# One 192-column PSUM bank for half B's three gate sums in a gated recurrent layer

## The chip, the cores and the metric

The kernel runs on one core of one Trainium2 chip. The metric is the device time of one execution in microseconds (us), and lower is better. Before the change it is 1670.06 us, the median of 3 runs.

## The reference

A gated recurrent layer walks 512 steps over 8 sequences of width 512, and its states are added to its input:

```python
def step(h, x_t):
    fused = sigmoid(concatenate([x_t, h], -1) @ w_W + w_b)
    hidden_state, output_state = split(fused, 2, axis=-1)          # r, z
    memory_state = x_t @ wx_W + wx_b + hidden_state * (h @ wh_W + wh_b)
    h_new = output_state * h + (1.0 - output_state) * tanh(memory_state)
    return (h_new, h_new)
return x + swapaxes(scan(step, h0, swapaxes(x, 0, 1))[1], 0, 1)
```

All arrays are float32: x is (8, 512, 512), w_W is (1024, 1024), wx_W and wh_W are (512, 512). The state of one step is needed by every product of the next one, so the steps form a chain.

## The kernel before

**Halves.** The 512 units lie as four chunks of 128. Chunks 0 and 1 are half A, chunks 2 and 3 half B. Each half has its own state tile (`hTA`, `hTB`), its own gates and its own place in the order of work. Three sums are wanted per step and half: hh (the product with wh_W), z and r, each 64 columns wide.

**TensorE.** For every step i the product of the state with the weights is issued as groups named by a bank and a chunk k of the state: A0 multiplies chunk 0 into bank A. A group is four matmuls, one for each j, and each writes 32 of the 128 output partitions, so four run beside each other. Each matmul of the program stands in the trace as two records (8176 records of `A<-wa,hTA` are 511 steps times 16, for the 8 matmuls of A0 and A1). Chunks 0 and 1 come from `hTA`, chunks 2 and 3 from `hTB`. The order is written out by hand:

```python
ORDER = "A0 B0 A1 A2 A3 B1 B2 B3 C0 C1 C2 C3"
BANKS = {"A": 192, "B": 128, "C": 64}
```

Bank A holds hh, z, r of half A (192 columns). For half B, bank B holds r and hh (128 columns) and bank C holds z (64 columns). After C3, `take(later, 7)` issues seven matmuls of 192 columns of the x side (tile `xp`), which belong to later steps and wait for no state. They are used up in steps 5 to 500; the last 11 steps have none, and steps 0 to 4 have wider ones of another kind (384 columns). `turn` rotates the order of j, so that the four strips share the x side evenly over the steps.

**VectorE and ScalarE.** Both work through a fixed order, the order of the source. In each step VectorE does, with the names of the trace:

1. half A: `tr<-A` (transpose of r), `md1A<-A` (of hh), `tz<-A` (of z), then two scans `m<-md0A,md1A` that make the memory state of chunks 0 and 1;
2. half B: `tr<-B`, `md1B<-B`;
3. the scan `hTA<-hd0A,hTA` of chunk 0, the new state that A0 and B0 of the next step wait for;
4. half B: `tz<-C`;
5. the scan `hTA` of chunk 1, then two scans `m` of half B and two scans `hTB`, for which A2 and A3 of the next step wait;
6. a few steps of upkeep (a transpose of the x side, memsets).

ScalarE takes the sigmoids (`md0A<-tr`, `hd0A<-tz` and the same for B) and the tanh (`hTA<-m`, `hTB<-m`) between them, and at the end of a step copies. A wait in this order holds up all that stands behind it on the engine. In the code the steps are `turn_r`, `turn_h`, `turn_z`, `memory` and `update`, each called for half 0 (A) and 1 (B); their transposes are recorded at L374 and L390, the scans at L358, the activations at L216, and every matmul at L188.

**Banks and spreads.** Each of the banks exists twice, and four steps (a group g) accumulate in one set. Before a group begins, `spread` copies the x part of its sums from `xp` (or from a copy in SBUF) into its banks on ScalarE (L251). There is one such copy for each bank and group. GpSimd adds x to the new state and SyncE stores the rows.

Of the kernel before, what the change touches and what calls it, by code (L numbers as in the profile page):

```python
# [16 lines left out]
B = 8  # L17
HU = 64
# [5 lines left out]
LAST = 4  # L24
SYNC = mybir.DependencyInfo(mybir.DependencyClass.Sync, mybir.DependencyReason.DATA)

ORDER = "A0 B0 A1 A2 A3 B1 B2 B3 C0 C1 C2 C3"

FIRST = "A0 x A1 x A2 x A3 B0 B1 B2 B3 C0 C1 C2 C3"

BANKS = {"A": 192, "B": 128, "C": 64}

HALF = 192

AL, BE = (0, slice(64, 256)), (0, slice(256, 448))
GA, DE = (1, slice(64, 256)), (1, slice(256, 448))

XP = {"A": slice(0, 192), "X": slice(192, 320), "C": slice(320, 384), "B": slice(384, 512)}


@with_exitstack
def tile_cond_rnn_residual(
# [84 lines left out]
    wa = const.tile([P, NQ, NQ, 192], F32, name="wa")  # L127
    for k in range(NQ):
        nc.sync.dma_start(out=wa[:, k], in_=wa_d[k])
    wb = const.tile([P, NQ, NQ, 192], F32, name="wb")  # L130
# [1 line left out]
    nc.sync.dma_start(out=wb[:, 3], in_=wb3_d)  # L132

    def wh(bank, k, j):
        return wa[:, k, j] if bank == "A" else wb[:, k, j, {"C": slice(0, 64), "B": slice(64, 192)}[bank]]

    load_x(0, 1)

# [36 lines left out]
    def state(hf, i, slot=2):  # L175
# [5 lines left out]
    banks = [  # L181
        {n: psum.tile([P, w], F32, name=f"{n}{q}") for n, w in BANKS.items()}
        for q in range(2)
# [3 lines left out]
    def mm(out_, lhsT, rhs, start=False):  # L187
        nc.tensor.matmul(  # L188
            out_, lhsT, rhs, start=start, stop=False, skip_group_check=True
        )  # L190
# [31 lines left out]
    def seed(g):  # L222

        nc.scalar.copy(xps[g % 2], bias)  # L224
# [19 lines left out]
    def part(g, c0, c1):  # L244

        return late(g)[:, c0 - 256 : c1 - 256] if c0 >= 256 else xps[g % 2][:, c0:c1]

    def spread(g, names):

        for n in names:  # L250
            nc.scalar.copy(banks[g % 2][n], part(g, XP[n].start, XP[n].stop))  # L251

    def turn_x(g, e):

        c0 = XP["X"].start + 32 * e
        nc.vector.transpose(md1[e // 2][g % 2][:, :, e % 2, 1], part(g, c0, c0 + 32))

    def reg(r):
        return xps[r[0]][:, r[1]]
# [8 lines left out]
    def weight_sum(n, k=slice(0, 2), j=None):  # L268

        a, b = [  # L270
            (wx_of(0, 1), wx_of(0, 0)),
            (wx_of(1, 1), tw[0]),
            (wx_of(1, 1), wx_of(0, 1)),
            (wx_of(1, 0), tw[1]),
        ][n]
        at = (slice(0, P), k, slice(0, NQ) if j is None else slice(2 * j, 2 * j + 2))
        nc.vector.tensor_tensor(tw[n][at], a[at], b[at], ALU.subtract)

    def x_sum(o, n):

        t_ = [q[o % 2] for q in sx]
        a, b, op = [
            (x_half(o, 1, 0), x_half(o, 1, 1), ALU.add),
            (t_[0], x_half(o, 0, 0), ALU.subtract),
            (x_half(o, 0, 0), x_half(o, 1, 0), ALU.subtract),
            (x_half(o, 0, 1), t_[1], ALU.subtract),
        ][n]
        nc.gpsimd.tensor_tensor(t_[n], a, b, op)
# [32 lines left out]
    first = {g: prefill(g) for g in (1, 2, 3)}  # L321
    weight_sum(0)
    weight_sum(2)
    spread(0, "BCA")
    for e in range(NQ):
        turn_x(0, e)

# [1 line left out]
    for i in range(T):  # L329
        g, s = divmod(i, GS)  # L330
        c, t = divmod(i, TC)
        ps = banks[g % 2]
# [4 lines left out]

        for n in (ORDER if i else FIRST).split():
            if n == "x":
                take(first[1], 1)  # L340
                continue
            bank, k = n[0], int(n[1])
            hs = hT[k // 2][i % NH][:, :, k % 2, 2]
            for j in range(NQ):
                j = (j + turn[0]) % NQ
                to = ps[bank] if i or bank != "A" else xps[0][:, XP["A"]]
                mm(to[32 * j : 32 * j + 32, :], hs, wh(bank, k, j))
# [8 lines left out]
        def scan(c_, out_, d0, d1):  # L356
# [7 lines left out]

        pa = ps["A"] if i else xps[0][:, XP["A"]]
        raw = {
            "h": (pa[:, :HU], ps["B"][:, HU:]),
            "z": (pa[:, HU : 2 * HU], ps["C"]),
            "r": (pa[:, 2 * HU :], ps["B"][:, :HU]),
        }  # L370

        def turned(n, hf):
# [82 lines left out]
        o, u = divmod(i, 2 * GS)  # L455
# [8 lines left out]
        if u == 0:  # L464
            spread(2 * o + 1, "B")
            if o and nxt:
                nc.scalar.copy(reg(GA), reg(BE))
        elif u == 1:
            spread(2 * o + 1, "C")
        elif u == 2 and o == 0:  # L470
            seed(3)
            nc.scalar.copy(even, xps[0][:, 256:512])
        elif u == 2 and nxt:
            last = odd[(o + 1) % 2][:, :HALF]
            nc.vector.tensor_tensor(last, reg(GA), both, ALU.add)
        elif u == 3 and nxt:
            if o:
                nc.vector.tensor_tensor(even[:, :HALF], reg(BE), both, ALU.add)
            spread(2 * o + 2, "A")
        elif u == 4 and nxt:  # L480
            if o == 0:
                nc.scalar.copy(odd[1], xps[1][:, 256:512])
            spread(2 * o + 2, "B")
            if two:
                nc.scalar.copy(reg(AL), bias[:, AL[1]])
                x_sum(o + 2, 0)
        elif u == 5 and nxt:
            spread(2 * o + 2, "C")
            if two:
                nc.scalar.copy(reg(DE), step_bias)  # L490
                x_sum(o + 2, 1)
        elif u == 6 and two:
            nc.scalar.copy(reg(BE), reg(AL))
            x_sum(o + 2, 2)
        elif u == 7 and nxt:
            spread(2 * o + 3, "A")
            if two:
                nc.scalar.copy(both, reg(DE))
                x_sum(o + 2, 3)
# [106 lines left out]
```

## Time and profile before

| what | value |
|---|---|
| median of 3 runs | 1670.06 us (1669.73 to 1671.35) |
| span of the profiled execution | 1670.8 us |
| granted TensorE clock, mean | 0.999 |
| PE busy / PEld busy | 1659.0 us (99%) / 1637.5 us (98%) |
| DVE busy / ACT busy | 1090.5 us (65%) / 1029.9 us (62%) |
| records of matmuls | 56238 |
| idle of DVE ahead of `tr<-A` | 463.5 us in 510 waits |

PE is the matmul side of TensorE and PEld its weight loads; DVE is VectorE, ACT ScalarE. The profiled execution has the span for its time; it is 0.8 us over the median of the runs. A busy PE is not a PE at its peak: the ends of matmuls are modelled and four of them overlap, so a wait of less than a matmul's length does not show as idle time. The starts in the timeline show it.

### The profile page before, as it was taken

What the parts mean: (1) busy time and instruction counts of PE and PEld (TensorE: products, weight loads), DVE (VectorE), ACT (ScalarE), POOL (GpSimd) and SP (SyncE); (2) the same over time, 40 slices, a digit from 0 to 9 for tenths busy, and PEclk for the clock granted to TensorE, in tenths of its full rate; (3) what the DMA queues carried; (4) which work ended last, traced back from release to release, by engine and by line L of the source; (5) the groups of instructions that cost most, each with busy time, mean ns of one, the idle gap of its engine ahead of it and who ended that gap; (6) DMA issues with size and microseconds to landing.
All of it is one profiled execution on the core that took longest, in us unless ns stands there. A gap on an engine that the chain in (4) does not pass through costs nothing.

```text
span 1670.8 us, 129875 instructions
## 1 busy us (share of the span) xinstructions
PE 1659.0 (99%) x56238; PEld 1637.5 (98%) x56238; DVE 1090.5 (65%) x9387; ACT 1029.9 (62%) x5822; POOL 301.9 (18%) x1281
## 2 busy tenths in 40 slices
PE   8999999999999999999999999999999999999998
PEld 5999999999999999999999999999999999999997
DVE  6666666666666666666666666666666666666666
ACT  3666666666666666666666666666666666666665
POOL 1111111111111111111111111111111111111111
PEclk9999999999999999999999999999999999999999
DMA  4000000000000000000000000000000000000000
GB/s 179 17 5 17 18 18 17 17 6 17 17 18 18 5 17 18 17 17 5 18 17 17 18 11 12 18 17 17 18 5 17 17 18 17 5 17 12 11 12 10
DMA packets 11525, 31.40 MB, mean 19 GB/s; under 512 B 1220, under 2 KB 1732, under 8 KB 10824
## 3 DMA queue, kind: packets, MB, share of 16 engines
q1 hardware_dynamic: 10800, 22.94, 4.0%
q8 instruction: 440, 7.21, 1.8%
q14 instruction: 133, 1.09, 0.2%
q10 hardware_dynamic: 152, 0.16, 0.0%
HBM read 14.70 MB, written 8.39 MB: 14 GB/s over the span
## 4 chain that ended last, share of the span: by engine, by line
PE 98%; DVE 1%; DMA 0%; issue 0%; ACT 0%
PE A L188 44%; PE B L188 23%; PE xp L188 20%; PE C L188 12%; DMA rows<-in_bias_dram 0%; DVE tr L374 0%; DVE m L358 0%; DVE tz L374 0%; DVE md1B L390 0%; DVE md1A L390 0%; DVE hTA L358 0%; DVE bias L203 0%; ACT hTB L216 0%; ACT xp L224 0%; DVE rows L120 0%
## 5 line engine op out<-in xcount | busy, mean ns | idle before, releaser
L188 PE MATMUL A<-wa,hTA 128*32 128x192 f32 x8176 | 638.2, 329 | 2.3 <-DVE hTA L358 2.3
L188 PE MATMUL B<-wb,hTA 128*32 128x128 f32 x8192 | 573.8, 273 | 0.0
L188 PE MATMUL A<-wa,hTB 128*32 128x192 f32 x8176 | 507.4, 326 | 0.5 <-DVE hTB L358 0.5
L188 PEld LDWEIGHTS B<-wb,hTA 128*32 128x32 f32 x8192 | 471.2, 122 | 1.4 <-issue 0.2
L374 DVE STREAM_TRANSPOSE tr<-A 128x64 f32<-128x64 f32 x511 | 127.7, 250 | 463.5 <-PE A L188 463.5
L188 PE MATMUL B<-wb,hTB 128*32 128x128 f32 x8192 | 398.9, 273 | 0.0
L188 PEld LDWEIGHTS A<-wa,hTA 128*32 128x32 f32 x8176 | 385.4, 123 | 7.6 <-DVE hTA L358 4.0
L188 PEld LDWEIGHTS A<-wa,hTB 128*32 128x32 f32 x8176 | 372.9, 122 | 2.7 <-DVE hTB L358 0.8
L216 ACT ACTIVATE md0A<-tr 128x16 f32<-128x16 f32 x512 | 112.3, 219 | 421.0 <-DVE tr L374 421.0
L507 POOL TENSOR_TENSOR ot<-xin,hTB 128x16 f32<-128x16 f32 x503 | 125.9, 250 | 1324.5 <-DVE hTB L358 1314.0
L188 PEld LDWEIGHTS B<-wb,hTB 128*32 128x32 f32 x8192 | 321.5, 122 | 0.1
L188 PE MATMUL C<-wb,hTA 128*32 128x64 f32 x8192 | 289.4, 219 | 0.0
L188 PE MATMUL C<-wb,hTB 128*32 128x64 f32 x8192 | 288.9, 220 | 0.2 <-issue 0.2
L188 PEld LDWEIGHTS C<-wb,hTA 128*32 128x32 f32 x8192 | 266.7, 122 | 0.0
L188 PE MATMUL xp<-tw,sx 128*32 128x192 f32 x2976 | 237.2, 326 | 0.1
L188 PEld LDWEIGHTS C<-wb,hTB 128*32 128x32 f32 x8192 | 229.2, 123 | 0.4 <-issue 0.4
L358 DVE TENSOR_TENSOR_SCAN hTB<-hd0B,hTB 128x24 f32<-128x24 f32 x1024 | 157.8, 195 | 101.0 <-ACT hTB L216 99.8
L358 DVE TENSOR_TENSOR_SCAN hTA<-hd0A,hTA 128x24 f32<-128x24 f32 x1024 | 191.0, 187 | 0.0
L188 PE MATMUL xp<-wx,xin 128*32 128x192 f32 (+1 forms) x2048 | 182.4, 331 | 0.7 <-issue 0.5
L216 ACT ACTIVATE hd0B<-tz 128x16 f32<-128x16 f32 x512 | 115.2, 225 | 93.7 <-DVE tz L374 93.7
L216 ACT ACTIVATE hTB<-hTB 128x16 f32<-128x16 f32 x512 | 120.5, 235 | 79.8 <-DVE hTB L358 72.3
L216 ACT ACTIVATE hTB<-m 128x8 f32<-128x8 f32 x1024 | 160.6, 206 | 0.0
(92 smaller groups left out, 2489.6 us busy)
## 6 DMA issues: line engine op xcount, KB each, us to landing
xin<-in_x_dram SPq DMA_DIRECT2D x31, 256.0 KB, 3.5
out_dram<-ot SPq DMA_DIRECT2D x31, 256.0 KB, 2.2
wx<-in_wx_dram SPq DMA_DIRECT2D x4, 768.0 KB, 7.1
wa<-in_wa_dram SPq DMA_DIRECT2D x4, 384.0 KB, 8.9
wb<-in_wb_dram SPq DMA_DIRECT2D x1, 1152.0 KB
wb<-in_wb_dram SPq DMA_DIRECT2D x1, 384.0 KB, 11.1
out_dram<-ot SPq DMA_DIRECT2D x1, 192.0 KB, 3.9
head<-in_xh_dram ACTq DMA_DIRECT2D x1, 144.0 KB, 5.0
```

Source lines behind the costliest of these rows:

```text
L188: nc.tensor.matmul(out_, lhsT, rhs, start=start, stop=False, skip_group_check=True)
L216: inst = nc.scalar.activation(out_, in_, func, **kw).ins
L358: return nc.vector.tensor_tensor_scan(*[t_[:, :, c_].rearrange("p n c s -> p (n c s)") for t_ in (out_, d0, d1)], 0.0, ALU.mult, ALU.add,).ins
L374: inst = nc.vector.transpose(t_.rearrange("p c n -> p (c n)"), raw[n][hf]).ins
L507: return engine.tensor_tensor(ot[:, t, 2 * hf : 2 * hf + 2, :].rearrange("p c n -> p n c"), x_of(c, slice(2 * hf, 2 * hf + 2), t, 1).rearr ...
```

## The change

Half B gets one bank of 192 columns, laid out z, r, hh, as wide as half A's. Bank C goes, and with it the groups C0 to C3 in both orders, the copies into C (128 in all, at steps 1 and 5 of every eight) and the entry for C in the map of `xp`. The matmuls of B are 192 columns wide instead of 128. `tz` of half B reads bank B. The order of all other work stays as it is written.

```diff
-ORDER = "A0 B0 A1 A2 A3 B1 B2 B3 C0 C1 C2 C3"
+ORDER = "A0 B0 A1 A2 A3 B1 B2 B3"
-FIRST = "A0 x A1 x A2 x A3 B0 B1 B2 B3 C0 C1 C2 C3"
+FIRST = "A0 x A1 x A2 x A3 B0 B1 B2 B3"
-BANKS = {"A": 192, "B": 128, "C": 64}
+BANKS = {"A": 192, "B": 192}
-XP = {"A": slice(0, 192), "X": slice(192, 320), "C": slice(320, 384), "B": slice(384, 512)}
+XP = {"A": slice(0, 192), "X": slice(192, 320), "B": slice(320, 512)}
...
-        return wa[:, k, j] if bank == "A" else wb[:, k, j, {"C": slice(0, 64), "B": slice(64, 192)}[bank]]
+        return (wa if bank == "A" else wb)[:, k, j]
...
-    spread(0, "BCA")
+    spread(0, "BA")
...
-            "h": (pa[:, :HU], ps["B"][:, HU:]),
-            "z": (pa[:, HU : 2 * HU], ps["C"]),
-            "r": (pa[:, 2 * HU :], ps["B"][:, :HU]),
+            "h": (pa[:, :HU], ps["B"][:, 2 * HU :]),
+            "z": (pa[:, HU : 2 * HU], ps["B"][:, :HU]),
+            "r": (pa[:, 2 * HU :], ps["B"][:, HU : 2 * HU]),
...
-        elif u == 1:
-            spread(2 * o + 1, "C")
...
-            spread(2 * o + 2, "C")
```

## The prediction

> **What bounds the kernel now.** I read the page's engine shares first, then the waits, then the timeline of single steps, because the first two cannot tell a full TensorE from one that waits in small pieces.
>
> ```profile
> span 1670.8 us, 129875 instructions
> PE 1659.0 (99%) x56238; PEld 1637.5 (98%) x56238; DVE 1090.5 (65%) x9387; ACT 1029.9 (62%) x5822; POOL 301.9 (18%) x1281
> ...
> DVE tr L374 <- PE A L188: 463.5, 510, 1.8
> PEld A L188 <- DVE hTA L358: 4.0, 11, 0.4
> ```
>
> PE is busy throughout, VectorE idles 463.5 / 510 = 0.91 us in each step before `tr<-A`, and TensorE is seen waiting for the state only 11 times. So TensorE's stream sets the time. The period of a step comes from two rows of the timeline, `tr<-A` of steps 5 and 501, with 496 periods between them.
>
> ```profile
> 38.15 0.25 DVE L374 STREAM_TRANSPOSE tr<-A 128x64 f32<-128x64 f32 x1 [1.22 <-PE A L188]
> ...
> 1635.05 0.25 DVE L374 STREAM_TRANSPOSE tr<-A 128x64 f32<-128x64 f32 x1 [0.97 <-PE A L188]
> ```
>
> (1635.05 - 38.15) / 496 = 3.220 us per step. From 1635.05 on there is no x side, and the ten periods up to the last `tr<-A` at 1665.83 (below) take 30.78 / 10 = 3.08 us. These last steps are the key to the case. TensorE has 7 matmuls (14 records) less in them, yet a step is only 0.14 us shorter: there the chain through VectorE and ScalarE sets the time. Here is one of them, from `tr<-A` to the next `tr<-A`.
>
> ```profile
> 1662.73 0.61 PE L188 MATMUL B<-wb,hTB 128*32 128x128 f32 x14
> 1662.75 0.25 DVE L374 STREAM_TRANSPOSE tr<-A 128x64 f32<-128x64 f32 x1 [0.94 <-PE A L188]
> 1663.16 0.41 PE L188 MATMUL C<-wb,hTA 128*32 128x64 f32 x16
> 1663.29 0.28 DVE L358 TENSOR_TENSOR_SCAN m<-md0A,md1A 128x16 f32<-128x16 f32 x2
> 1663.38 0.41 PE L188 MATMUL C<-wb,hTB 128*32 128x64 f32 x16
> 1663.48 0.23 DVE L374 STREAM_TRANSPOSE tr<-B 128x64 f32<-128x64 f32 x1
> 1663.63 0.21 DVE L390 STREAM_TRANSPOSE md1B<-B 128x64 f32<-128x64 f32 x1
> 1663.77 0.20 DVE L358 TENSOR_TENSOR_SCAN hTA<-hd0A,hTA 128x24 f32<-128x24 f32 x1
> 1663.88 0.23 DVE L374 STREAM_TRANSPOSE tz<-C 128x64 f32<-128x64 f32 x1
> 1664.02 0.19 PEld L188 LDWEIGHTS A<-wa,hTA 128*32 128x32 f32 x8 [0.39 <-DVE hTA L358]
> 1664.02 0.55 PE L188 MATMUL A<-wa,hTA 128*32 128x192 f32 x8 [0.24 <-DVE hTA L358]
> 1664.03 0.17 DVE L358 TENSOR_TENSOR_SCAN hTA<-hd0A,hTA 128x24 f32<-128x24 f32 x1
> 1664.23 0.30 PEld L188 LDWEIGHTS B<-wb,hTA 128*32 128x32 f32 x8
> 1664.50 0.25 PEld L188 LDWEIGHTS A<-wa,hTA 128*32 128x32 f32 x8
> 1664.56 0.31 DVE L358 TENSOR_TENSOR_SCAN hTB<-hd0B,hTB 128x24 f32<-128x24 f32 x2 [0.20 <-ACT hTB L216]
> 1664.82 0.58 PEld L188 LDWEIGHTS A<-wa,hTB 128*32 128x32 f32 x16
> 1664.93 0.83 PE L188 MATMUL A<-wa,hTB 128*32 128x192 f32 x16
> 1665.58 0.40 PE L188 MATMUL B<-wb,hTA 128*32 128x128 f32 x8
> 1665.83 0.25 DVE L374 STREAM_TRANSPOSE tr<-A 128x64 f32<-128x64 f32 x1 [0.95 <-PE A L188]
> 1666.24 0.41 PE L188 MATMUL C<-wb,hTA 128*32 128x64 f32 x16
> ```
>
> The chain is `tr<-A` at 1662.75, the scan of `hTA` at 1663.77, the weights of A0 at 1664.02 (1.27 after `tr<-A`), the last matmul of A3 ending at 1664.93 + 0.83 = 1665.76, and `tr<-A` 0.07 later: 1.27 + 1.74 + 0.07 = 3.08. The reader should note that the scan ends at 1663.97 and the weight load follows 0.05 later. A step in the middle of the run has the same front part:
>
> ```profile
> 802.27 0.25 DVE L374 STREAM_TRANSPOSE tr<-A 128x64 f32<-128x64 f32 x1 [1.02 <-PE A L188]
> 803.28 0.20 DVE L358 TENSOR_TENSOR_SCAN hTA<-hd0A,hTA 128x24 f32<-128x24 f32 x1
> 803.54 0.31 PEld L188 LDWEIGHTS A<-wa,hTA 128*32 128x32 f32 x8
> 803.56 0.33 PE L188 MATMUL xp<-wx,sx 128*32 128x192 f32 x2
> ```
>
> Again 803.54 - 802.27 = 1.27 us, 0.06 behind the end of the scan, with x-side matmuls still starting at 803.56. So in the steady state the first weights of A0 are loaded as soon as the state permits, while the x side still fills the other strips. The two limits, stream and chain, lie close together; the chain has about 0.1 us to spare.
>
> **The stream, part by part.** I call four records, one on each strip of 32 partitions, a round. The 16 records of A on `hTB` are four rounds from 1664.93 to 1665.58: 0.163 us a round of 192 columns. The 24 records of B1 to B3 are six rounds from 1665.58 to 1666.24: 0.110 us at 128 columns. The 16 of C on `hTA` are four rounds from 1663.16 to 1663.38: 0.055 us at 64. A B round of 192 columns and the B and C rounds it replaces therefore cost 0.163 against 0.165. Per step 8 rounds of C go (0.44), and 8 rounds of B grow by 0.053 (0.42). TensorE's work shrinks by 0.01 to 0.02 us a step, 32 records and 32 weight loads though it is. Rounding leaves a fixed cost per record between 0 and some 5 ns.
>
> The Trainium skill ("TensorE: Matmul & The Clock Gate", section "Wait — 56ns, not 53.3ns?") names about 2.5 ns fixed per warm matmul. By that rule the eight rounds would give 0.020 us a step, 10 us in all, if TensorE stayed the bound. The rows above cannot tell 1 ns from 2.5, and agree with it in size.
>
> The same skill's "TensorEngine Tiling (Array Packing)", section "Instruction Overhead", says that a matmul costs some 60 cycles however few its columns, which would make 64-column matmuls nearly pure overhead and the merge a large gain. The trace disagrees: 64 columns take 0.055 and 128 take 0.110, in proportion.
>
> **What moves.** The important part is when bank B is complete. Now B1 to B3 end at 1662.73 + 0.61 = 1663.34, well before `tr<-B` at 1663.48, which waits only for VectorE's scans `m`. After the change the z columns are streamed inside B1 to B3 instead of behind them. The last of six rounds starts five times 0.053 later and lasts 0.05 longer, so B ends 0.32 later, at 1663.66. `tr<-B` needs all of bank B. How long it takes from the end of the matmuls to the transpose is shown twice: 0.07 for `tr<-A` above, and in step 0, the only step in which `tr<-B` waited for its matmuls:
>
> ```profile
> 18.46 0.69 PE L188 MATMUL B<-wb,hTB 128*32 128x128 f32 x16
> 19.21 0.25 DVE L374 STREAM_TRANSPOSE tr<-B 128x64 f32<-128x64 f32 x1
> 19.52 0.17 DVE L358 TENSOR_TENSOR_SCAN hTA<-hd0A,hTA 128x24 f32<-128x24 f32 x1
> ```
>
> There it is 19.21 - 19.15 = 0.06, and the scan of `hTA` comes 0.31 behind `tr<-B`, against 1663.77 - 1663.48 = 0.29 where VectorE didn't wait; I take 0.07 and 0.31. `tr<-B` then starts at 1663.73, 0.25 late, and the scan at 0.25 + 0.02 = 0.27 late. Queued behind the waiting `tr<-B` on VectorE are `md1B`, that scan, `tz` of B, the second scan of `hTA`, and all of half B. The order puts the new state of half A behind half B's transposes, so half A, whose inputs are ready, pays for half B's bank.
>
> Next, the release of A0: 1.27 + 0.27 = 1.54 us after `tr<-A`. Would TensorE still have work then? Counted from `tr<-A`: B1 starts 0.25 before it (1665.58 against 1665.83), six rounds of 0.163 take it to 0.73, and four rounds of x side (14 records, so two or four for each strip) to 1.38. Even the strips with most work stand idle for 0.16 us, all four begin A0 together, and the weights aren't loaded ahead: the pattern of the last ten steps. So I take those steps as the template for every step, with A0 0.27 later and B0 of the next step, in front of A1, wider by two rounds of 0.053:
>
> - period: 3.08 + 0.27 + 0.105 = 3.455 us;
> - 496 steps with x side: 496 x (3.455 - 3.220) = 116.6 us;
> - the last ten periods: 10 x (3.455 - 3.08) = 3.8 us; the tail behind the last `tr<-A` 0.3 us;
> - steps 0 to 4 with their wider x side take over 3.9 us now, more than 3.455, so TensorE covers the delay there, at 0.
>
> Sum 120.7 us: 1670.8 + 120.7 = 1791.5 us, and against the median, 0.8 us lower, 1790.7. I forecast 1790.
>
> **What I cost at nothing.** The copies into C go (128 of them, ScalarE, behind the last state of the step) and those into B grow; ScalarE has more idle time than now, and if that cover went, some 0.05 us in every fourth step. A1 waits for the second scan of `hTA`, 1664.03 + 0.17 + 0.27 and 0.06 = 1664.53; its load would come at 1664.50 + 0.27, hidden by 0.24. A2 waits for `hTB`: even the later scan ends at 1664.87 + 0.27, so 1665.20 with the 0.06; its load comes at 1664.82 + 0.27 + 0.11 = 1665.20, just hidden, and the first scan, which is what A2 needs, is earlier. A new wait: B0 writes the bank from which `tz` of B still reads. `tz` would start at 1663.88 + 0.27 and end at 1664.38, 1664.44 with the 0.06; B0's load is due at 1664.23 + 0.27 = 1664.50. It is hidden by 0.06 us, the thinnest cover of all.
>
> On that wait the Trainium skill speaks against the change: "PSUM — Partial Sum Buffer", section "PSUM bank collisions raise a hardware error", has software guard a bank as a whole, so z in the same bank holds back all of B0 and not just z's columns. No row of before shows this wait.
>
> **The rivals.**
>
> 1. *TensorE stays the bound, faster.* Place: the x side between B3 and A0. If A0's state came by 1.38 us after `tr<-A`, the strips would not wait, and only the saved 0.01 to 0.02 us a step would be left: 1660 to 1665 us. It decides if the scan is less than 0.11 us late. For it speaks that the waits show no late state now; against it the sum of 0.27, and that TensorE does stop for 0.24 us in the last steps. Chance 0.04, and 0.01 that it ends within 0.2% of before.
> 2. *The chain is the bound but shorter.* If VectorE follows bank B by 0.04 instead of 0.07, and the strips don't fall into step, so that weights are loaded ahead (in the last steps the A0 records of two rounds and their restart take 1664.39 - 1664.02 = 0.37 to the first of B instead of 2 x 0.163, 0.04 more), the period is 0.07 to 0.09 lower: about 1750 us. Chance 0.13.
> 3. *The new wait of B0 shows.* If the guard against `tz` also keeps the loads behind it from being queued, a cover of 0.06 becomes a stall of about that size, 0.06 x 506 = 30 us: 1820 us. Chance 0.07.
>
> **How the numbers follow.** The forecast has 0.75; with 0.03 us either way on the period it spans 1775 to 1805. The range reaches into rival 2 and toward rival 3: 1748 to 1815. What one measurement can tell from no change is 0.2%, 3.3 us; faster 0.04, same 0.01, slower 0.95.
>
> **What would show it.** In the new profile `tr<-B` should have a wait for PE B in nearly every step and start 0.97 to 1.0 us after `tr<-A` (now 0.73), A0's weights should come at 1.54 (now 1.27) with an idle put down to `hTA`, `tr<-A` should follow itself at 3.45 with and without x side, and the rounds of B should be 0.163. If `tr<-B` waits but the period stays below 3.25, the spare time of the stream was larger than I read; if `tr<-B` doesn't wait, my end of bank B is wrong; if `B` waits for `tz`, rival 3 is at work.

## The result and the profile after

The changed kernel takes 1774.51 us (median of 4 runs, 1773.87 to 1775.2) against 1670.7 us for the kernel before (median of 4 runs, three of which are those behind the 1670.06 us above): a ratio of 1.0617, 95% interval 1.0602 to 1.0632. It is slower, as forecast, by 104 us where the forecast had 120. The two profiled spans differ by 1771.5 - 1670.8 = 100.7 us.

First the page of the changed kernel, then three lines of its waits (us in total, times, longest):

```profile
span 1771.5 us, 96975 instructions
...
PE 1755.4 (99%) x39852; PEld 1370.5 (77%) x39852; DVE 1145.0 (65%) x9387; ACT 1084.1 (61%) x5694; POOL 305.1 (17%) x1281
...
DVE tr L374 <- PE A L188: 427.3, 510, 1.0
PEld A L188 <- DVE hTA L358: 171.1, 507, 1.0
DVE tr L374 <- PE B L188: 83.8, 511, 1.5
```

PE is still 99% busy, with 16386 records of matmuls fewer and 100 us more time: that share cannot tell a stream from a stream with holes, since each matmul's modelled length overlaps its neighbours. The weight loads can. PEld fell from 98% to 77%, and it now waits for the new state of half A in 507 steps instead of 11. `tr<-B` waits for bank B in 511 steps, 0.16 us each; the waits of the kernel before list none for bank B.

One of the last steps in the timeline, which corresponds to the step shown for the kernel before:

```profile
1762.85 0.25 DVE L374 STREAM_TRANSPOSE tr<-A 128x64 f32<-128x64 f32 x1 [1.01 <-PE A L188]
1762.92 0.83 PE L188 MATMUL B<-wb,hTB 128*32 128x192 f32 x16
1763.38 0.28 DVE L358 TENSOR_TENSOR_SCAN m<-md0A,md1A 128x16 f32<-128x16 f32 x2
1763.82 0.25 DVE L374 STREAM_TRANSPOSE tr<-B 128x64 f32<-128x64 f32 x1 [0.16 <-PE B L188]
1763.99 0.21 DVE L390 STREAM_TRANSPOSE md1B<-B 128x64 f32<-128x64 f32 x1
1764.12 0.17 DVE L358 TENSOR_TENSOR_SCAN hTA<-hd0A,hTA 128x24 f32<-128x24 f32 x1
1764.21 0.22 DVE L374 STREAM_TRANSPOSE tz<-B 128x64 f32<-128x64 f32 x1
1764.34 0.19 PEld L188 LDWEIGHTS A<-wa,hTA 128*32 128x32 f32 x8 [0.96 <-DVE hTA L358]
1764.55 0.31 PEld L188 LDWEIGHTS B<-wb,hTA 128*32 128x32 f32 x8
1765.20 0.63 PEld L188 LDWEIGHTS A<-wa,hTB 128*32 128x32 f32 x16
1766.26 0.25 DVE L374 STREAM_TRANSPOSE tr<-A 128x64 f32<-128x64 f32 x1 [1.01 <-PE A L188]
```

Read it from the top. The two scans `m` of half A are over at 1763.66, VectorE stands for 0.16 us until `tr<-B` can start at 1763.82, 0.07 behind the end of the last matmul of bank B (1762.92 + 0.83 = 1763.75), and only then come `md1B` and, third in line, the scan that makes half A's state. A0's weights are loaded at 1764.34, 1.49 us after `tr<-A` (1.27 before). From there to the next `tr<-A` it takes 1.92 us (1.81 before, as B0 now sits there 64 columns wider). 1.49 + 1.92 = 3.41 us is the period, and it is the same with x side: from 38.27 (step 5) to 1732.11 (step 501), 496 periods of 3.415 us.

```profile
38.27 0.25 DVE L374 STREAM_TRANSPOSE tr<-A 128x64 f32<-128x64 f32 x1 [0.94 <-PE A L188]
...
1732.11 0.25 DVE L374 STREAM_TRANSPOSE tr<-A 128x64 f32<-128x64 f32 x1 [0.89 <-PE A L188]
```

### The profile page after: what moved, and what is told of

It reads as the page before. It is cut to its first block, busy times and chain, and to the rows that moved or that the text cites. A ratio compares the mean times of both kernels' runs of the same rounds, so it can differ in the third digit from the quotient of the medians.

```text
span 1771.5 us, 96975 instructions
## 1 busy us (share of the span) xinstructions
PE 1755.4 (99%) x39852; PEld 1370.5 (77%) x39852; DVE 1145.0 (65%) x9387; ACT 1084.1 (61%) x5694; POOL 305.1 (17%) x1281
## 4 chain that ended last, share of the span: by engine, by line
PE 98%; DMA 1%; DVE 0%; ACT 0%; issue 0%
PE A L188 42%; PE B L188 38%; PE xp L188 18%; DMA wb<-in_wb_dram 1%; DMA rows<-in_bias_dram 0%; DVE tr L374 0%; DVE md1B L390 0%; DVE hTA L358 0%; ACT hTB L216 0%; ACT xp L224 0%; DVE rows L120 0%; DVE hTB L358 0%; DVE tz L374 0%; ACT hd0B L216 0%; ACT hTA L216 0%
## 5 line engine op out<-in xcount | busy, mean ns | idle before, releaser
L188 PE MATMUL A<-wa,hTA 128*32 128x192 f32 x8176 | 539.4, 336 | 5.9 <-DVE hTA L358 5.9
L188 PE MATMUL B<-wb,hTA 128*32 128x192 f32 x8192 | 520.5, 326 | 0.8 <-DMA wb<-in_wb_dram 0.8
L188 PE MATMUL B<-wb,hTB 128*32 128x192 f32 x8192 | 426.7, 326 | 0.0
L188 PEld LDWEIGHTS A<-wa,hTA 128*32 128x32 f32 x8176 | 241.6, 124 | 194.3 <-DVE hTA L358 171.1
L188 PEld LDWEIGHTS A<-wa,hTB 128*32 128x32 f32 x8176 | 289.8, 122 | 42.8 <-DVE hTB L358 0.9
L188 PEld LDWEIGHTS B<-wb,hTA 128*32 128x32 f32 x8192 | 289.7, 122 | 42.0 <-DMA wb<-in_wb_dram 1.1
L374 DVE STREAM_TRANSPOSE tr<-B 128x64 f32<-128x64 f32 x512 | 128.0, 250 | 83.8 <-PE B L188 83.8
L216 ACT ACTIVATE md0B<-tr 128x16 f32<-128x16 f32 x512 | 111.2, 217 | 95.0 <-DVE tr L374 94.9
L216 ACT ACTIVATE hTA<-m 128x8 f32<-128x8 f32 x1024 | 160.6, 206 | 0.0
L358 DVE TENSOR_TENSOR_SCAN m<-md0A,md1A 128x16 f32<-128x16 f32 x1024 | 142.0, 181 | 4.4
```

The lines of the kernel that those rows point to most:

```text
L188: nc.tensor.matmul(out_, lhsT, rhs, start=start, stop=False, skip_group_check=True)
L216: inst = nc.scalar.activation(out_, in_, func, **kw).ins
L358: return nc.vector.tensor_tensor_scan(*[t_[:, :, c_].rearrange("p n c s -> p (n c s)") for t_ in (out_, d0, d1)], 0.0, ALU.mult, ALU.add,).ins
L374: inst = nc.vector.transpose(t_.rearrange("p c n -> p (c n)"), raw[n][hf]).ins
```

## The experiments

Below, *release* is the time from `tr<-A` to the first weights of A0 in the next step, and *rest* the time from there to the next `tr<-A`. Theory: the period is the larger of release + rest (the chain) and what TensorE's stream of matmuls needs (the stream), and the change lengthened the release through the late completion of bank B. In the comparisons of this section the kernel before took 1684 to 1688 us and not 1670.7, so each ratio is to the kernel before on the same chip, and absolute times written down beforehand are some 15 us low where the stream decides.

### The same order of columns, with two banks

```diff
-ORDER = "A0 B0 A1 A2 A3 B1 B2 B3 C0 C1 C2 C3"
+ORDER = "A0 B0 C0 A1 A2 A3 C1 C2 C3 B1 B2 B3"
```

> The kernel before with its two banks B (128) and C (64) for half B, but with TensorE's groups in the order A0 B0 C0 A1 A2 A3 C1 C2 C3 B1 B2 B3, which is where the changed kernel has the same columns. Bank B is then complete as late as in the changed kernel, with narrow matmuls and z in a bank of its own. Theory (the loss is the later completion of bank B, which holds up VectorE's transpose of r of half B and, queued behind it, the new state of half A): period about 3.43 us, time about 1784 us (1770 to 1795), tr<-B about 0.99 us after tr<-A. Rival (the shared bank or the 192-column matmuls cost by themselves): near the kernel before, 1670 to 1690 us.

1784.31 us, ratio 1.0593 (1.0576 to 1.0609). Its timeline in the last steps:

```profile
1772.33 0.25 DVE L374 STREAM_TRANSPOSE tr<-A 128x64 f32<-128x64 f32 x1 [1.02 <-PE A L188]
1773.32 0.25 DVE L374 STREAM_TRANSPOSE tr<-B 128x64 f32<-128x64 f32 x1 [0.18 <-PE B L188]
1773.62 0.17 DVE L358 TENSOR_TENSOR_SCAN hTA<-hd0A,hTA 128x24 f32<-128x24 f32 x1
1773.84 0.19 PEld L188 LDWEIGHTS A<-wa,hTA 128*32 128x32 f32 x8 [0.85 <-DVE hTA L358]
1775.77 0.25 DVE L374 STREAM_TRANSPOSE tr<-A 128x64 f32<-128x64 f32 x1 [1.02 <-PE A L188]
```

`tr<-B` comes 0.99 after `tr<-A`, release 1.51, rest 1.93, together 3.44. Nothing of the change is in this kernel but the place of z's columns, and practically the whole loss is there (a ratio of 1.0593, for 1.0617 of the changed kernel). So the loss needs neither the shared bank nor the wide matmuls; the order of the columns makes it.

### Bank C in front of B1 to B3, all of it or half

```diff
-ORDER = "A0 B0 A1 A2 A3 B1 B2 B3 C0 C1 C2 C3"
+ORDER = "A0 B0 A1 A2 A3 C0 C1 C2 C3 B1 B2 B3"
```

> The kernel before with all of bank C ahead of B1: A0 B0 A1 A2 A3 C0 C1 C2 C3 B1 B2 B3. Bank B is complete 0.44 us later. Theory: tr<-B at about 1.10 us after tr<-A, A0's weights at about 1.63 us, past the 1.49 at which the stream is free, all strips stand; period 3.43 us, about 1782 us (1765 to 1795). Rival (shared bank, width): no change, 1670 us.

1784.81 us, ratio 1.0597 (1.058 to 1.0614).

```profile
1773.57 0.25 DVE L374 STREAM_TRANSPOSE tr<-A 128x64 f32<-128x64 f32 x1 [0.91 <-PE A L188]
1774.67 0.25 DVE L374 STREAM_TRANSPOSE tr<-B 128x64 f32<-128x64 f32 x1 [0.29 <-PE B L188]
1775.19 0.19 PEld L188 LDWEIGHTS A<-wa,hTA 128*32 128x32 f32 x8 [0.85 <-DVE hTA L358]
1777.01 0.25 DVE L374 STREAM_TRANSPOSE tr<-A 128x64 f32<-128x64 f32 x1 [0.91 <-PE A L188]
```

`tr<-B` at 1.10, release 1.62, and the rest is back at 1.82, for B0 is 128 columns wide here and nothing else was put ahead of A1. Against 1.92 of the changed kernel this measures the second term alone: 0.10 us for the wider B0.

With half of bank C in front, bank B is complete 0.22 us later instead of 0.44:

```diff
-ORDER = "A0 B0 A1 A2 A3 B1 B2 B3 C0 C1 C2 C3"
+ORDER = "A0 B0 A1 A2 A3 C0 C1 B1 B2 B3 C2 C3"
```

> The kernel before with two of bank C's four groups moved ahead of B1: A0 B0 A1 A2 A3 C0 C1 B1 B2 B3 C2 C3. Bank B is complete 0.22 us later, nothing else changes. Theory with the stream's spare time: tr<-B starts 0.88 to 0.91 us after tr<-A (0.73 before), the weights of A0 come at about 1.40 us, and the strips with most work are free only at about 1.49, so the delay is covered: 1670 to 1680 us. If there is no spare time and each delay of the state is paid in full: 0.13 us x 506, about 1736 us.

1695.94 us, ratio 1.0072 (1.0051 to 1.0093): small, but no tie, and in absolute time above the 1670 to 1680 us written down, where the kernel before is 14 us slower as well.

```profile
38.44 0.25 DVE L374 STREAM_TRANSPOSE tr<-A 128x64 f32<-128x64 f32 x1 [1.05 <-PE A L188]
...
1653.10 0.25 DVE L374 STREAM_TRANSPOSE tr<-A 128x64 f32<-128x64 f32 x1 [0.83 <-PE A L188]
...
1682.01 0.25 DVE L374 STREAM_TRANSPOSE tr<-A 128x64 f32<-128x64 f32 x1 [0.90 <-PE A L188]
1682.89 0.25 DVE L374 STREAM_TRANSPOSE tr<-B 128x64 f32<-128x64 f32 x1
1683.41 0.19 PEld L188 LDWEIGHTS A<-wa,hTA 128*32 128x32 f32 x8 [0.52 <-DVE hTA L358]
1685.22 0.25 DVE L374 STREAM_TRANSPOSE tr<-A 128x64 f32<-128x64 f32 x1 [0.91 <-PE A L188]
```

Here the two limits part. In the last steps, without x side, the chain is 1.40 + 1.81 = 3.21 us and that is the period. In steps 5 to 501 the period is (1653.10 - 38.44) / 496 = 3.255: there the chain is no longer the limit. Of a release 0.13 us later only (1695.94 - 1684.15) / 506 = 0.023 us a step is paid; from half to all of bank C, 0.22 us more of release cost 0.18. That anything is paid shows that the larger of two limits is a little too simple where they lie this close: counted record by record in the traces, from step 100 to 400, a strip stands idle ahead of A0 for 0.058 us a step on average, and for 0.021 in the kernel before.

### The scan of half A moved up on VectorE, in the changed kernel

```diff
         turn_r(1)
+        update(0, 0)
         turn_h(1)
-        update(0, 0)
         turn_z(1)
```

> The changed kernel with one step moved on VectorE: the first scan of hTA, update(0, 0), between the transposes of r and of hh of half B instead of behind both. Theory (half A's state waits behind half B's transposes): A0's weights come at about 1.35 us after tr<-A instead of 1.50, TensorE is no longer held at A0, and what is late next is hTB for A2; period 3.20 to 3.30 us, 1670 to 1715 us. Rival (shared bank or wide matmuls by themselves): unchanged, about 1774 us. Rival (B0's new wait for tz of half B is what holds TensorE): A0 is earlier but B0 is not, 1740 us or more, with an idle before B0's weights.

1708.43 us, ratio 1.0141 (1.0126 to 1.0157).

```profile
843.18 0.25 DVE L374 STREAM_TRANSPOSE tr<-A 128x64 f32<-128x64 f32 x1 [0.77 <-PE A L188]
844.16 0.25 DVE L374 STREAM_TRANSPOSE tr<-B 128x64 f32<-128x64 f32 x1 [0.16 <-PE B L188]
844.33 0.17 DVE L358 TENSOR_TENSOR_SCAN hTA<-hd0A,hTA 128x24 f32<-128x24 f32 x1
844.55 0.19 PEld L188 LDWEIGHTS A<-wa,hTA 128*32 128x32 f32 x8 [0.19 <-DVE hTA L358]
844.57 0.20 DVE L374 STREAM_TRANSPOSE tz<-B 128x64 f32<-128x64 f32 x1
844.82 0.24 PEld L188 LDWEIGHTS B<-wb,hTA 128*32 128x32 f32 x8
844.92 0.51 PE L188 MATMUL B<-wb,hTA 128*32 128x192 f32 x8
846.47 0.25 DVE L374 STREAM_TRANSPOSE tr<-A 128x64 f32<-128x64 f32 x1 [0.54 <-PE A L188]
```

One scan moved by one place brings the ratio from 1.0617 down to 1.0141. Release 1.37, 0.13 less than in the changed kernel, rest 1.92 as there, period 3.29: the chain term for term, and 0.13 x 506 = 66 us is what the time fell by (1774.51 to 1708.43, in two comparisons). In these rows the new wait of B0 is seen too: its weights come at 844.82, 0.05 behind the end of `tz<-B` at 844.77. But its first matmul starts at 844.92, 0.37 behind A0's weights, just as in the last steps of the kernel before (1664.02 to 1664.39); the wait is there and costs nothing.

### A second move in the changed kernel, and both moves in the kernel before

The two scans `m` of half B were put ahead of the second scan of `hTA` as well.

```diff
         turn_r(1)
+        update(0, 0)
         turn_h(1)
-        update(0, 0)
         turn_z(1)
-        tc.add_manual_dep(update(0, 1), r_done[1].name, SYNC)
+        memory(1, 0)
+        memory(1, 1)
+        update(0, 1)
...
-        memory(1, 0)
-        memory(1, 1)
         update(1, 0)
```

> The changed kernel with two moves on VectorE: the first scan of hTA directly behind tr of half B (as in the run with one move), and the two scans m of half B ahead of the second scan of hTA, update(0, 1). Theory: A0's weights at about 1.35 us after tr<-A, the scans m of half B some 0.12 us earlier and with them hTB, so that A2 comes in time; the stream sets the time again, period 3.17 to 3.23 us, 1650 to 1685 us. If the shared bank costs (B0 waits for tz of half B): an idle of 0.05 to 0.1 us before B0's weights in each step, 1690 to 1720 us.

1709.38 us, ratio 1.0141 (1.0111 to 1.017): no better than the first move alone, a miss. The scans of `hTB` start 2.03 us after `tr<-A` (843.08 to 845.11) instead of 2.08 (843.18 to 845.26), but they were not what held A2's matmuls. With a release of 1.37 and ten rounds of 192 columns behind it (A0, B0, A1, A2, A3) the chain is 3.29 us whatever `hTB` does.

> The kernel before with the same two moves on VectorE. Theory: its stream already sets the time, with 0.02 to 0.03 us a step lost at A0 in one strip; period 3.19 to 3.22 us, 1655 to 1672 us. It tells how much of a gain of the moved changed kernel is the order and how much the single bank.

1695.35 us, ratio 1.0057 (1.0035 to 1.0079), a miss: slightly slower, not faster. The rows of a late step show what it costs, counted from `tr<-A` at 1680.84: the second scan of `hTA` starts at 1.65 (1.28 in the step shown for the kernel before), A1's weights come at 1.89 instead of 1.75, 0.05 behind its end, and `hTB` gains nothing, 1.93 against 1.81. How much of this is paid in the steps with x side was not taken apart.

> The kernel before with one step moved on VectorE: the first scan of hTA between the transposes of r and hh of half B. Theory (period is the larger of the chain, A0's release + 1.81 us, and TensorE's stream): A0's weights come at about 1.20 instead of 1.27 us after tr<-A, limited by the tanh of half A; the chain in the last ten steps falls from 3.08 to about 3.01 us; with x side the stream sets the time and only the small wait of one strip at A0 goes: 0 to 0.5% faster than the kernel before, as the run without recurrence allowed (0.997). Rival (the chain still sets the time of the kernel before): faster by 0.07 us a step, 2%.

1689.43 us against 1688.07, ratio 1.0007 (0.9994 to 1.0019): no change, and the release did not move.

```profile
1675.48 0.25 DVE L374 STREAM_TRANSPOSE tr<-A 128x64 f32<-128x64 f32 x1 [0.88 <-PE A L188]
1676.24 0.31 ACT L216 ACTIVATE hTA<-m 128x8 f32<-128x8 f32 x2
1676.49 0.21 DVE L358 TENSOR_TENSOR_SCAN hTA<-hd0A,hTA 128x24 f32<-128x24 f32 x1
1676.75 0.19 PEld L188 LDWEIGHTS A<-wa,hTA 128*32 128x32 f32 x8 [0.39 <-DVE hTA L358]
1677.42 0.31 DVE L358 TENSOR_TENSOR_SCAN hTB<-hd0B,hTB 128x24 f32<-128x24 f32 x2 [0.19 <-ACT hTB L216]
1677.68 0.51 PEld L188 LDWEIGHTS A<-wa,hTB 128*32 128x32 f32 x16 [0.20 <-DVE hTB L358]
1678.62 0.25 DVE L374 STREAM_TRANSPOSE tr<-A 128x64 f32<-128x64 f32 x1 [0.88 <-PE A L188]
```

The scan still starts 1.01 after `tr<-A`, as before: in this kernel the tanh of half A on ScalarE is ready only then (the first of the two ends at 1676.45). VectorE's order costs half A nothing as long as bank B is complete in time. The chain of the last steps was expected to fall to 3.01 us; it rose from 3.08 to 3.14. Half B's work now stands behind the scan that waits for the tanh: `hTB` starts 1.94 after `tr<-A` instead of 1.81, and A2's weights wait for it. With x side, where the stream decides, this costs nothing that can be measured. No version with the recurrence that was tried beats the kernel before.

### TensorE without the recurrence

```diff
+    fixed = [pair(n, f"fixed{n}", 32, 3) for n in "AB"]
+    for t_ in fixed:
+        nc.gpsimd.memset(t_, 0.01)
...
-            hs = hT[k // 2][i % NH][:, :, k % 2, 2]
+            hs = fixed[k // 2][:, :, k % 2, 2]
```

> The kernel before with the state products taken from a constant tile instead of the state (the recurrence is left out of the matmuls; all other work stays), so TensorE never waits for the state: its stream alone. From the rounds of the trace (0.1625, 0.109, 0.056): period 3.19 us, about 1655 us.

1680.63 us, ratio to the kernel before 0.9971 (0.9951 to 0.999). The state costs the kernel before 0.3%: it was bound by its stream, as the prediction said. The 1655 us that I had from the rounds were missed by 25 us, and the miss is in the period: `tr<-A` goes from 37.72 (step 5) to 1644.60 (step 501), 3.24 us a step against the 3.19 of the rounds, and 0.05 x 506 = 25. Counted record by record, more than half of the strips' idle time lies ahead of the records of C. Some 15 of the 25 us the kernel before shows too between the comparisons; why the strips stand was not settled.

> The changed kernel with the state products taken from a constant tile (the recurrence is left out of the matmuls; all other work stays). Stream alone: 0.02 us a step less than the same for the kernel before, period 3.17 us, about 1645 us. If B0's wait for tz of half B is a bound of its own, the period is above that, 3.20 us or more, with idle before B0's weights.

1679.68 us, ratio 0.9958 (0.9943 to 0.9973), the same as the other within their intervals. Three records in ten less (39852 for 56238) buy nothing that can be measured here. The timeline shows why:

```profile
902.40 0.21 PEld L191 LDWEIGHTS B<-wb,fixedA 128*32 128x32 f32 x8
...
903.99 0.25 DVE L377 STREAM_TRANSPOSE tr<-A 128x64 f32<-128x64 f32 x1 [0.71 <-PE A L191]
905.36 0.22 DVE L377 STREAM_TRANSPOSE tz<-B 128x64 f32<-128x64 f32 x1
905.63 0.22 PEld L191 LDWEIGHTS B<-wb,fixedA 128*32 128x32 f32 x8
905.63 0.58 PE L191 MATMUL B<-wb,fixedA 128*32 128x192 f32 x8
```

With the state out of the way, B0 is held until z of half B is read: its first weights come 0.05 behind the end of `tz<-B` (905.58) and its first matmul in the same moment. The shared bank does have a limit of its own, 905.63 - 902.40 = 3.23 us a step here, but it lies well under the 3.41 that decides in the changed kernel. The trace bears it out record by record, from step 100 to 400: the 78 records of a step, 0.1625 us each on four strips, take 78 x 0.1625 / 4 = 3.169 us, and a strip stands idle 0.064 us on average, all of it ahead of B0; together that is the period.

The Trainium skill's rule ("PSUM — Partial Sum Buffer", section "PSUM bank collisions raise a hardware error") has software guard PSUM by bank and quadrant (32 partitions), in its simple version by bank, and not by address. These rows fit it but do not test it: every matmul of B0 writes all 192 columns, z's among them, so a guard of z's columns alone would hold B0 as well.

## Why the prediction was right, point by point

- **TensorE's stream bound the kernel before; the chain bounds the kernel after.** Held: 0.997 without the state before, and 3.41 us with and without x side after.
- **`tr<-B` 0.97 to 1.0 us after `tr<-A`.** Measured 0.97 (1763.82 - 1762.85), with a wait for B in 511 steps.
- **The rest wider by 0.105.** Measured 1.92 against 1.81, and 0.10 between the changed kernel and the run with all of bank C in front.
- **The release 0.27 later, 1.54.** This is the term that was mis-sized: it is 1.49 to 1.50. The scan does start 0.30 behind `tr<-B`, but lasts 0.17 instead of 0.20 us, as its inputs have long been there; I had let its end move as far as its start. 0.04 x 506 = 20 us, and 1791.5 - 20 is the measured span of 1771.5. With the measured period of 3.415 in place of 3.455 the prediction's own sum closes: 96.7 + 3.4 + 0.3 = 100.4 us, where the spans differ by 100.7.
- **B0's new wait for `tz`.** Held in the changed kernel (weights at 1764.55, `tz<-B` over at 1764.43), no cover was lost; two runs showed the wait itself. That a guard of the whole bank matters for it, as the prediction has it, no run shows.
- **Rivals 2 and 3.** Neither came about. `tr<-B` follows the end of bank B by 0.07 us, not by 0.04, and from A0's first matmul to B0's it takes 0.36 us (1764.35 to 1764.71), so the strips do fall into step; B0's wait costs nothing here.
- **Rival 1's decisive point.** Wrong, though the rival did not come about. I wrote that a state at 1.38 us would leave TensorE the bound, 1660 to 1665 us. The run with one scan moved has it at 1.37 and takes 1708 us, because the chain's rest is then 1.92 and the sum 3.29. The point should have been taken from release + rest against the stream's 3.2, that is at about 1.3.
- **The saved fixed cost per matmul.** The 0.01 to 0.02 us a step could not be collected in any run: without the state the two kernels take the same time, and the changed one then waits at B0. In the spacing of the records it is there: in the kernel before, records on one strip follow each other by 0.1625 us at 192 columns, 0.109 at 128 and 0.056 at 64, so 128 and 64 apart take 0.0025 us more than 192 together. The 2.5 ns of the Trainium skill ("TensorE: Matmul & The Clock Gate", section "Wait — 56ns, not 53.3ns?") agree with that. The estimate of 10 us that follows from them no run shows as time.
- **The overhead that was ruled out.** A fixed cost for each matmul would make the merge a large gain only if it were large and added to every matmul. The rows exclude such an addition, as 64 and 128 columns stand in proportion (0.056 and 0.109 us). A least time for still narrower matmuls is not tested here.

## What to carry to other kernels

When two accumulators are merged, the one that was needed early becomes as late as the one that could wait; look at who waits for the merged bank and at what stands behind that wait in an engine's fixed order, here the state of the other half. Steps at the end of a run that lack the filler work show the bare chain, and the chain plus the moved waits gives the new period before the change is run, here to within 0.04 us. A share of 99% busy on overlapping matmuls is not a limit reached; ask instead in how many steps the weight loads stand idle for the new state (11 before, 507 after). That the first weight load follows the state at once is not enough: it did so in the kernel before too (803.54, 0.06 behind the scan), with other strips still at work.

## What the runs showed that had not been expected

In the rows shown, the first scan of `hTA` lasts 0.20 to 0.21 us where its input came just before and 0.17 us where it had been ready. Fewer and wider matmuls gained nothing that could be measured: 16386 records less, 1679.68 against 1680.63 us with the state left out, where the wait at B0 takes what the spacing of the records would save. The kernel before, bound by its stream, took 1670.7 us in one comparison and 1684 to 1688 us in the others; why was not taken apart.
